# Layer 3 of a four-layer graph network: scaled rows and 512-column matmuls in place of scaled one-hots, radial weights per node tile

## The chip, the cores and the metric

The kernel runs on one core of a Trainium2 chip. The core has five engines with a queue of instructions each: TensorE (PE; its weight loads are shown apart as PEld), VectorE (DVE), ScalarE (ACT), GpSimd (POOL) and SyncE (SP), which here only issues DMAs. An engine executes its own queue in order and waits on semaphores for the others. Arrays live in the device's HBM; the engines work on SBUF (128 partitions) and PSUM (the matmuls' output). The metric is the time of one execution in microseconds (us), lower is better.

## The reference

A graph of 3125 nodes with 256 features and 50,000 edges, whose edges come sorted by target (`dst`), goes through four layers, each followed by a residual and a layer norm. Layers 0 (attention), 1 (attention over the graph, with a dense exponential) and 2 (two hypergraph convolutions) are not changed. Layer 3 is what the change rewrites:

```python
src = node_in[edge_src]
s0 = src[:, :MUL]                          # MUL = 64
s1 = src[:, MUL:].reshape(-1, MUL, 3)
a0 = edge_attr[:, 0:1]
a1 = edge_attr[:, 1:4]
out0 = alpha * (jnp.einsum('ei,io->eo', s0 * a0, w_00_0) + inv_sqrt3 * jnp.einsum('eim,em,io->eo', s1, a1, w_11_0))
out1 = alpha * (jnp.einsum('ei,io,em->eom', s0, w_01_1, a1) + jnp.einsum('eim,io->eom', s1 * a0[:, :, None], w_10_1))
msg_ang = jnp.concatenate([out0, out1.reshape(-1, 3 * MUL)], axis=1)
h = jax.nn.silu(edge_len_emb @ fc_w1 / np.float32(np.sqrt(10.0))) * np.float32(SILU_NORM)
msg_rad = h @ fc_w2 / np.float32(np.sqrt(64.0))
messages = msg_ang * msg_rad
agg = jax.ops.segment_sum(messages, edge_dst, num_segments=node_in.shape[0])
return agg / np.float32(np.sqrt(NUM_NEIGHBORS))
```

Each edge takes the row of its source node (one part of 64 features, three parts of 64), multiplies it with four numbers of the edge (`edge_attr`, 50,000 x 4) and with one number, the radial weight, that a small network makes of ten more (`edge_len_emb`, here `edge_attr_10`). Products of the row's parts with the four numbers go through 64 x 64 matrices and are added up over the edges of each target node. The matrices don't depend on the edge, so the sum can be taken first.

## The kernel before

**Node tiles and slots.** The 3125 nodes are 25 tiles of 128 (`NN = 25`). As edges are sorted by target, the edges of a node tile are a run that begins at a place read at run time (`self.at[t]`); the kernel takes `CAP = 2176` edges from there, as 128 partitions of `S = 17` slots. `one_hot` (L1002 to 1007) makes, for each slot, the 128 x 128 matrix that says which edge belongs to which node of the tile; a matmul with it as weights adds edges up over nodes.

**Gathers and fills.** `gather` (L86) is an indirect DMA that GpSimd issues: 128 rows of a table by an index per partition. A tile needs 17, in layer 0's attention (`kv`) as in layer 3 (`g`). `fill` (L1073) issues, also on GpSimd, scatters into `mat`, the matrix of edge counts of layers 1 and 2: 391 of them for the first of two matrices, eight per node tile inside the attention loop. They need only `put0` and `count`, which `counts` (L1010) makes, and the cleared matrix.

**What sets the order.** The code is one trace through Python; a planner then lays out each engine's queue. It estimates when an instruction's inputs and memory are ready and takes the earliest traced of those that are. So an instruction that is ready may go into the queue ahead of one that was traced before it. `attend` pins its gathers, the reads of `mine` and the first fill of each eight behind what was traced before them on GpSimd (`keep_in_program_order`, L1075 to 1082 and L1187 to 1194); the other seven fills of eight are not held by that, since two fills need no order between them. Memory is planned too: pools opened one after another share the same SBUF addresses, and a tile waits until those that lie on its place are done. `project_all`, `counts`, `edge_weights` and the attention of layer 0 are traced in this order (L1664 to 1667), and their pools share a region.

**Radial weights before.** `edge_weights` (L1558) calls `radial` (L119 to 143), which computes the radial weight of all 391 x 128 edges in one go, eight edge tiles at a time, and multiplies `edge_attr_4` with it:

```python
for i in range(n):
    nc.tensor.matmul(hp[:, i, :], emb[:, i * P:(i + 1) * P], w1, start=True, stop=True)
hs = sp.tile([P, B, F], F32, name="rad_h")
nc.scalar.activation(hs[:, :n], hp[:, :n], AF.Silu, scale=1.0 / math.sqrt(10.0))
nc.vector.tensor_mul(hs[:, :n], hs[:, :n], w2[:, None, :].to_broadcast([P, n, F]))
nc.vector.tensor_reduce(rad[:, j0:j0 + n], hs[:, :n], AX.X, ALU.add)
```

These are lines 136 to 141. The products are then turned by matmuls with the identity (L1570), copied (L1572) and stored as rows in HBM (`e_w4`, L1573), from where layer 3 loads 17 x 4 numbers per partition and tile (L1598).

**Layer 3 before.** Layer 2's last step writes each finished node tile into a table (`l3_tab`, by `l3_row`, L1579). Layer 3 gathers the 17 rows per partition of a tile (L1614 to 1616; three buffers `g3`), makes the one-hot (L1617, one buffer), and for each slot multiplies the one-hot on VectorE with each of the four weighted numbers (`ws`, L1622). Four matmuls per slot then use these as weights: one of 256 columns into `acc0` (L1624) and three of 128 columns into `acc1` (L1627), 640 columns in all. After 17 slots the sums are copied to SBUF (L1630, 1631), turned in five pieces (L1634), copied (L1636), multiplied with five blocks of the 64 x 64 matrices (`blk`, L1639), added to the residual (L1641, 1642), normed (`layernorm`, L1122) and stored (L1648).

**Attention in layer 0.** `attend` (L1173) gathers kv rows in halves of nine and eight slots (`fetch`, five buffers of 18.3 KB a partition), makes scores on PE and VectorE (L1222, 1224), reads back the scores of its nodes (`mine`, L1234), issues its fills, and after three tiles runs the feed-forward part (L1315).

Of the kernel before, what the change touches and what calls it, by code (L numbers as in the profile page):

```python
# [8 lines left out]
F32 = mybir.dt.float32  # L9
# [3 lines left out]
AF = mybir.ActivationFunctionType  # L13
# [5 lines left out]
P = 128  # L19
# [957 lines left out]
class Sorted(General):  # L977
# [580 lines left out]
    def edge_weights(self):  # L1558

        nc, tc = self.nc, self.tc  # L1560
        rows = self.dram.tile([EL, 4], F32, name="e_w4")
        with tc.tile_pool(name="ew", bufs=1) as cp, tc.tile_pool(name="ews", bufs=2) as sp, \
                tc.tile_pool(name="ewp", bufs=2, space=PSUM) as pp:
            w = cp.tile([P, NT, 4], F32, name="wts")
            self.radial(w)
            for c in range(LCH):
                n = min(P, NT - c * P)
                tp = pp.tile([P, 4, P], F32, name="w4_p")
                for i in range(4):
                    nc.tensor.transpose(tp[:n, i, :], w[:, c * P:c * P + n, i], self.ident)  # L1570
                o = sp.tile([P, P, 4], F32, name="w4")
                nc.scalar.copy(o[:n].rearrange("r p i -> r i p"), tp[:n])  # L1572
                nc.sync.dma_start(rows[c * P * P:(c * P + n) * P, :].rearrange("(r p) i -> r p i", p=P), o[:n])  # L1573
            z = cp.tile([ER - NT, P * 4], F32, name="zw")
            nc.vector.memset(z, 0.0)
            nc.sync.dma_start(rows[EP:, :].rearrange("(r p) i -> r (p i)", p=P), z)
        return rows
# [10 lines left out]
    def layer3(self, tab, rows, out):  # L1588
        nc, tc, a = self.nc, self.tc, self.a
        M = 64  # L1590
        alpha = 1.0 / math.sqrt(2.0 * M)
        with ExitStack() as at:
            pool = lambda n, b, **k: at.enter_context(tc.tile_pool(name=n, bufs=b, **k))
            cp, gp, sp, wp = pool("l3c", 1), pool("l3g", 3), pool("l3s", 2), pool("l3ws", 1)
            ap, pp = pool("l3a", 2, space=PSUM), pool("l3p", 1, space=PSUM)
            w4 = cp.tile([P, NN, S, 4], F32, name="w4_n")
            for t in range(NN):
                nc.sync.dma_start(w4[:, t], rows[bass.ds(self.at[t], CAP), :].rearrange("(p s) k -> p s k", s=S))  # L1598

            blk = cp.tile([P, 5, D], F32, name="blk")  # L1600
            nc.vector.memset(blk, 0.0)
            put = lambda i, half, col, n: nc.sync.dma_start(
                blk[half * M:(half + 1) * M, i, col * M:(col + 1) * M], a["L3_gnn_" + n])
            put(0, 0, 0, "w_00_0")
            put(0, 1, 1, "w_10_1")
            put(1, 0, 2, "w_10_1")
            put(1, 1, 3, "w_10_1")
            for m in range(3):
                put(2 + m, 0, 1 + m, "w_01_1")
                put(2 + m, 1, 0, "w_11_0")  # L1610
            nc.vector.tensor_scalar(blk, blk, alpha, None, op0=ALU.mult)
            nc.vector.tensor_scalar(blk[M:, 2:, :], blk[M:, 2:, :], 1.0 / math.sqrt(3.0), None, op0=ALU.mult)
            for t in range(NN):
# [3 lines left out]
                oh = self.one_hot(wp, t)  # L1617
                acc0 = ap.tile([P, D], F32, name="acc0")
                acc1 = ap.tile([P, 3, 2, M], F32, name="acc1")
                for s in range(S):  # L1620
                    ws = sp.tile([P, 4, P], F32, name="ws")
                    nc.vector.tensor_tensor(ws, oh[:, s, None, :].to_broadcast([P, 4, P]),  # L1622
                                            w4[:, t, s, :, None].to_broadcast([P, 4, P]), op=ALU.mult)
                    nc.tensor.matmul(acc0, ws[:, 0, :], g[:, s, :], start=(s == 0), stop=(s == S - 1))  # L1624
                    gb = g[:, s, :].rearrange("p (b c) -> p b c", c=M)
                    for m in range(3):
                        nc.tensor.matmul(acc1[:, m], ws[:, 1 + m, :], gb[:, 0:m + 2:m + 1, :],  # L1627
                                         start=(s == 0 and m == 0), stop=(s == S - 1 and m == 2))
                sums = sp.tile([P, 5, P], F32, name="sums3")
                nc.scalar.copy(sums[:, :2, :].rearrange("p a b -> p (a b)"), acc0)  # L1630
                nc.scalar.copy(sums[:, 2:, :], acc1.rearrange("p m b c -> p m (b c)"))
                tp = pp.tile([P, 5, P], F32, name="tp3")
                for i in range(5):
                    nc.tensor.transpose(tp[:, i, :], sums[:, i, :], self.ident)  # L1634
                st = sp.tile([P, 5, P], F32, name="st3")
                nc.scalar.copy(st, tp)  # L1636
                o = pp.tile([P, D], F32, name="o3")
                for i in range(5):
                    nc.tensor.matmul(o, st[:, i, :], blk[:, i, :], start=(i == 0), stop=(i == 4))  # L1639
# [5 lines left out]
                y = sp.tile([P, D], F32, name="y3")  # L1645
                self.layernorm(sp, y, x)
                n = min(P, N - t * P)
                nc.sync.dma_start(out[t * P:t * P + n, :], y[:n, :])  # L1648


    def run(self, out):
# [10 lines left out]
        with tc.tile_pool(name="w0", bufs=1) as self.wp:  # L1662
            qw = self.load_qkv(0)
            self.project_all(qw)  # L1664
            self.counts()
            rows = self.edge_weights()
            self.layer0(qw)
# [6 lines left out]
        with tc.tile_pool(name="xp", bufs=1) as xp:  # L1674
# [5 lines left out]
            self.layer3(tab, rows, out)  # L1680
# [159 lines left out]
```

## Time and profile before

| what | value |
|---|---|
| median of 3 runs | 5379.77 us (5369.6 to 5383.34) |
| the profiled execution | 5377.31 us, span of its profile 5375.0 us |
| granted PE clock, mean over the span | 0.843 |
| PE / DVE / ACT / POOL busy | 4066.3 / 2816.2 / 1385.3 / 2373.8 us |
| radial's matmuls (L137, 782) | 167.1 us, between 511 and 678 us |
| attention of layer 0, both passes | first kv gather at 765.7, last at 2928.5 us |
| layer 3 | first gather at 4761.0, last at 5357.8 us |
| DMA queue of GpSimd's indirect transfers | 115824 packets, 287.06 MB |

Busy time is the time in which an engine executes an instruction; waits, semaphores and the issuing of DMAs by SP and ACT are not counted. A row of a group of instructions reads: line, engine, operation, what it writes and reads, count, then busy time and mean length of one in ns, then the time that the engine stood idle just before them and what ended it. A row in order of time reads: start, length (us), engine, line, operation, tiles, count, and in brackets the idle time before. A row by stretches reads: the stretch, its length, busy time and count, granted clock, share of the DMA engines and GB/s. The chain of waits is followed back from the last instruction, at each step to what released it; "issue" is time in which the engine waited for nothing that the profile shows.

### The profile page before, as it was taken

To read this page: it belongs to the slowest core of one execution; us is meant where nothing else is said; L and a number is where in the kernel's file an instruction comes from. 1 tells how busy PE (TensorE), PEld (TensorE's weight loads), DVE (VectorE), ACT (ScalarE), POOL (GpSimd) and SP (SyncE) were. 2 spreads that over 40 slices of the span, in tenths; PEclk is the share of its full clock that TensorE was granted. 3 is DMA by queue.
4 is the path that set the end of the run, shared out by engine and by line. 5 is a ranking of instruction groups with operands and counts; after the bars stand their busy time and mean duration, and the time that the engine had idled before them with its cause. 6 is when DMAs were issued, how large, how long until landed. Compare 5 with 4: busy or idle time off the path is not lost. (4 is left out here: it accounts for less than half of the span.)

```text
span 5375.0 us, 59023 instructions
## 1 busy us (share of the span) xinstructions
PE 4066.3 (76%) x21215; PEld 2838.4 (53%) x21215; DVE 2816.2 (52%) x5251; ACT 1385.3 (26%) x2412; POOL 2373.8 (44%) x2116
## 2 busy tenths in 40 slices
PE   2631925557777776777777899897799999979998
PEld 1321914435555555556556643233466566568888
DVE  3424415436666656656667257988511211356665
ACT  1110101212222220222112257877652111100000
POOL 0001777764545517545554048787100000047776
PEclk9765556768888887788788679998999999989999
DMA  3244024234444426444554112221233333323333
GB/s 89 76 189 180 13 66 140 75 100 148 150 145 148 147 81 210 140 150 150 162 153 130 32 45 67 62 69 43 75 90 92 99 88 98 109 84 100 98 101 90
DMA packets 341121, 575.18 MB, mean 107 GB/s; under 512 B 101939, under 2 KB 238958, under 8 KB 340817
## 3 DMA queue, kind: packets, MB, share of 16 engines
q0 software_dynamic: 115824, 287.06, 18.5%
q1 hardware_dynamic: 219234, 243.28, 15.0%
q10 hardware_dynamic: 5760, 40.96, 1.9%
q8 instruction: 171, 2.80, 0.2%
q14 instruction: 132, 1.08, 0.1%
HBM read 485.82 MB, written 85.24 MB: 106 GB/s over the span
## 5 line engine op out<-in xcount | busy, mean ns | idle before, releaser
L87 POOL DMA_INDIRECT kv<-kv,src_i x850 | 933.7, 1098 | 695.8 <-issue 228.8
L1077 POOL DMA_INDIRECT mat<-count,put x782 | 907.9, 1161 | 509.7 <-DMA put<-put1d 231.6
L87 POOL DMA_INDIRECT g<-l_tab,src_i x425 | 469.0, 1103 | 1103.5 <-issue 1097.7
L1222 PE MATMUL qe<-q,oht 128*128 128x256 bf16 x2550 | 423.0, 316 | 431.1 <-DVE kv L1224 414.7
L1444 PE MATMUL acc<-e,xe 128*65 128x512 f32 (+2 forms) x1600 | 579.5, 516 | 80.9 <-DVE e L1441 80.6
L1222 PEld LDWEIGHTS <-oht 128*128 128x128 bf16 x2550 | 321.3, 147 | 590.9 <-issue 536.2
L1271 PE MATMUL acc<-kv,oh 128*128 128x264 f32 x1700 | 443.7, 424 | 65.3 <-DVE kv L1269 65.3
L1444 PEld LDWEIGHTS acc<-e,xe 128*65 128x65 f32 x1600 | 213.4, 141 | 436.8 <-issue 298.4
L1271 PEld LDWEIGHTS acc<-kv,oh 128*128 128x128 f32 x1700 | 354.9, 211 | 145.6 <-DVE kv L1269 76.5
L1495 PE MATMUL cv<-parts,m 128*128 128x512 bf16 x1250 | 411.4, 380 | 14.9 <-DMA m<-mat 14.7
L1495 PE MATMUL cv<-mids,m 128*128 128x512 bf16 x1250 | 408.4, 379 | 10.6 <-DVE y L1517 9.5
L1441 DVE TENSOR_TENSOR e<-e,m 128x1280 f32<-128x1280 f32 (+1 forms) x300 | 370.0, 1264 | 70.0 <-DMA m<-mat 54.6
L1495 PEld LDWEIGHTS <-m 128*128 128x128 bf16 x2500 | 244.7, 98 | 301.6 <-issue 16.1
L1622 DVE TENSOR_TENSOR ws<-oh,w_n 128x512 f32<-128x512 f32 x425 | 291.5, 691 | 159.7 <-PE acc L1627 153.6
L1224 DVE TENSOR_TENSOR kv<-kv,qe 128x512 f32<-128x512 f32 (+1 forms) x450 | 286.4, 648 | 168.6 <-DMA kv<-kv,src_i 140.5
L1627 PEld LDWEIGHTS acc<-g,ws 128*128 128x128 f32 x2550 | 352.7, 192 | 22.1
L1627 PE MATMUL acc<-g,ws 128*128 128x128 f32 x2550 | 354.1, 275 | 0.0
L1497 PE MATMUL cv<-mids,m 128*128 128x256 bf16 x1250 | 338.9, 273 | 0.0
L1497 PE MATMUL cv<-parts,m 128*128 128x256 bf16 x1250 | 338.6, 273 | 0.0
L1440 ACT ACTIVATE e<-e 128x1280 f32<-128x1280 f32 (+1 forms) x300 | 316.8, 1086 | 77.9 <-DVE e L1438 74.9
L1624 PE MATMUL acc<-g,ws 128*128 128x256 f32 x850 | 267.1, 396 | 47.2 <-DMA g<-l_tab,src_i 33.3
L137 PE MATMUL rad_p<-fc,emb 10*128 10x64 f32 x782 | 167.1, 416 | 163.3 <-DMA fc<-in_L_gnn_fc_w 163.3
(253 smaller groups left out, 5932.6 us busy)
## 6 DMA issues: line engine op xcount, KB each, us to landing
m<-mat SPq DMA_DIRECT2D x550, 160.0 KB
mat<-zmat ACTq DMA_DIRECT2D x40, 1000.0 KB
m<-mat SPq DMA_DIRECT2D x100, 320.0 KB
keys<-e_dst SPq DMA_DIRECT2D x50, 544.0 KB
q<-q SPq DMA_DIRECT2D x100, 192.0 KB
kv<-kv,src_i POOLq DMA_INDIRECT x850
kv<-qkv SPq DMA_DIRECT2D x50, 256.0 KB
mat<-count,put POOLq DMA_INDIRECT x782
```

What stands on the lines that cost most here:

```text
L87: return self.nc.gpsimd.indirect_dma_start(out=out, out_offset=None, in_=table, in_offset=bass.IndirectOffsetOnAxis(ap=idx, axis=0))
L1077: ins = nc.gpsimd.indirect_dma_start(out=self.mats[i], out_offset=bass.IndirectOffsetOnAxis(ap=put[:, j - j0:j - j0 + 1], axis=0), in_=sel ...
L1222: nc.tensor.matmul(qe[:, u, :], slots[:, h0 + s0 + u, :], q[:, k, :], start=(k == 0), stop=(k == 2))
L1224: nc.vector.tensor_mul(kv[:, s0:s0 + n, :D], kv[:, s0:s0 + n, :D], qe[:, :n, :])
L1271: nc.tensor.matmul(acc, oh[:, s, :], kv[:, s, D:], start=(h0 + s == 0), stop=(h0 + s == S - 1))
L1440: nc.scalar.activation(e[:, :R], e[:, :R], AF.Exp, scale=0.8)
L1441: nc.vector.tensor_mul(e[:, :R], e[:, :R], m[:, :R])
L1444: nc.tensor.matmul(accs[h, c][:, :n], xe[:, t, h, :], e[:, c:c + n], start=(t == 0), stop=(t == NN - 1))
L1495: nc.tensor.matmul(accs[i], block, parts[:, b, :2, :].rearrange("p a f -> p (a f)"), start=(b == 0), stop=False)
L1497: nc.tensor.matmul(accs[i][:, :D], block, parts[:, b, 2, :], start=False, stop=(b == NN - 1))
L1622: nc.vector.tensor_tensor(ws, oh[:, s, None, :].to_broadcast([P, 4, P]), w4[:, t, s, :, None].to_broadcast([P, 4, P]), op=ALU.mult)
L1627: nc.tensor.matmul(acc1[:, m], ws[:, 1 + m, :], gb[:, 0:m + 2:m + 1, :], start=(s == 0 and m == 0), stop=(s == S - 1 and m == 2))
```

## The change

- `edge_weights` becomes `edge_attributes`: radial is not called any more. `edge_attr_4` itself is turned and stored as rows (`e_attr`), and `edge_attr_10` is copied from HBM to a padded array in HBM (`e_emb`, ten rows).
- In layer 3 each node tile loads its own ten embedding rows, six times over with a shift of one edge, as 60 partitions of 2176 numbers, so that one matmul with a block-diagonal weight (`w1`, 60 x 6 x 64) gives the hidden layer of six slots; three such matmuls, three Silu, a product with `w2` and a reduction give the 17 radial weights per partition. They multiply the tile's `edge_attr` numbers.
- The gathered rows are scaled instead of the one-hots: ScalarE multiplies each slot's 256 features with the first number; VectorE forms the scalar part times the three others, and the three other parts times the three others, added up to one. The eight parts of 64 make a row of 512 columns (`y`), and one matmul per slot with the plain one-hot as weights adds it up.
- After the sum there are four pieces instead of five to be turned and multiplied.

```diff
-    def edge_weights(self):
-
-        nc, tc = self.nc, self.tc
-        rows = self.dram.tile([EL, 4], F32, name="e_w4")
+    def edge_attributes(self):
+
+        nc, tc, a = self.nc, self.tc, self.a
+        self.attr = self.dram.tile([EL, 4], F32, name="e_attr")
+        self.emb = self.dram.tile([10, EL], F32, name="e_emb")
+        run = EP // S
+        nc.sync.dma_start(self.emb[:, :EP].rearrange("r (s e) -> r s e", e=run),
+                          a["edge_attr_10"].rearrange("r (s e) -> r s e", e=run))
...
-            w = cp.tile([P, NT, 4], F32, name="wts")
-            self.radial(w)
+            w = cp.tile([P, NT, 4], F32, name="attr")
+            nc.sync.dma_start(w, a["edge_attr_4"])
...
-    def layer3(self, tab, rows, out):
+    def layer3(self, tab, out):
...
-            cp, gp, sp, wp = pool("l3c", 1), pool("l3g", 3), pool("l3s", 2), pool("l3ws", 1)
-            ap, pp = pool("l3a", 2, space=PSUM), pool("l3p", 1, space=PSUM)
-            w4 = cp.tile([P, NN, S, 4], F32, name="w4_n")
-            for t in range(NN):
-                nc.sync.dma_start(w4[:, t], rows[bass.ds(self.at[t], CAP), :].rearrange("(p s) k -> p s k", s=S))
+            cp, gp, yp, sp = pool("l3c", 1), pool("l3g", 3), pool("l3y", 2), pool("l3s", 2)
+            op = pool("l3o", 1)
+            ap, rp, pp = pool("l3a", 2, space=PSUM), pool("l3r", 2, space=PSUM), pool("l3p", 1, space=PSUM)
...
+            w1 = cp.tile([10 * U, U, F], F32, name="fc1")
+            nc.vector.memset(w1, 0.0)
+            for i in range(U):
+                nc.sync.dma_start(w1[10 * i:10 * (i + 1), i, :], a["L3_gnn_fc_w1"])
+            w2 = self.bcast(cp, a["L3_gnn_fc_w2"], F, "fc2")
...
-                oh = self.one_hot(wp, t)
-                acc0 = ap.tile([P, D], F32, name="acc0")
-                acc1 = ap.tile([P, 3, 2, M], F32, name="acc1")
+
+                emb = sp.tile([10 * U, CAP], F32, name="emb")
+                run = self.emb[:, bass.ds(self.at[t], CAP)]
+                nc.sync.dma_start(emb, bass.AP(tensor=run.tensor, offset=run.offset,
+                                               ap=[[1, U], [EL, 10], [1, CAP]]))
+                slots = emb.rearrange("k (p s) -> k s p", s=S)
+                hs = sp.tile([P, S, F], F32, name="rad_h")
+                for s0 in range(0, S, U):
+                    n = min(U, S - s0)
+                    hp = rp.tile([P, U, F], F32, name="rad_p")
+                    nc.tensor.matmul(hp[:, :n], slots[:10 * n, s0, :],
+                                     w1[:10 * n, :n, :].rearrange("k u f -> k (u f)"), start=True, stop=True)
+                    nc.scalar.activation(hs[:, s0:s0 + n], hp[:, :n], AF.Silu, scale=1.0 / math.sqrt(10.0))
+                nc.vector.tensor_mul(hs, hs, w2[:, None, :].to_broadcast([P, S, F]))
+                rad = sp.tile([P, S], F32, name="rad")
+                nc.vector.tensor_reduce(rad, hs, AX.X, ALU.add)
+                w4 = sp.tile([P, S, 4], F32, name="w4")
+                nc.sync.dma_start(w4, self.attr[bass.ds(self.at[t], CAP), :].rearrange("(p s) k -> p s k", s=S))
+                nc.vector.tensor_mul(w4, w4, rad[:, :, None].to_broadcast([P, S, 4]))
+
+                y = yp.tile([P, S, 8 * M], F32, name="y")
                 for s in range(S):
-                    ws = sp.tile([P, 4, P], F32, name="ws")
-                    nc.vector.tensor_tensor(ws, oh[:, s, None, :].to_broadcast([P, 4, P]),
-                                            w4[:, t, s, :, None].to_broadcast([P, 4, P]), op=ALU.mult)
-                    nc.tensor.matmul(acc0, ws[:, 0, :], g[:, s, :], start=(s == 0), stop=(s == S - 1))
-                    gb = g[:, s, :].rearrange("p (b c) -> p b c", c=M)
-                    for m in range(3):
-                        nc.tensor.matmul(acc1[:, m], ws[:, 1 + m, :], gb[:, 0:m + 2:m + 1, :],
-                                         start=(s == 0 and m == 0), stop=(s == S - 1 and m == 2))
+                    nc.scalar.activation(y[:, s, :D], g[:, s, :], AF.Copy, scale=w4[:, s, 0:1])
+                a1 = w4[:, :, 1:, None].to_broadcast([P, S, 3, M])
+                nc.vector.tensor_mul(y[:, :, 4 * M:7 * M].rearrange("p s (m c) -> p s m c", c=M),
+                                     g[:, :, None, :M].to_broadcast([P, S, 3, M]), a1)
+                s1 = g[:, :, M:].rearrange("p s (m c) -> p s m c", c=M)
+                nc.vector.tensor_mul(s1, s1, a1)
+                nc.vector.tensor_add(y[:, :, 7 * M:], s1[:, :, 0], s1[:, :, 1])
+                nc.vector.tensor_add(y[:, :, 7 * M:], y[:, :, 7 * M:], s1[:, :, 2])
+                oh = self.one_hot(op, t)
+                acc = ap.tile([P, 8 * M], F32, name="acc3")
+                for s in range(S):
+                    nc.tensor.matmul(acc, oh[:, s, :], y[:, s, :], start=(s == 0), stop=(s == S - 1))
```

`blk`, `sums`, `tp`, `st` and the output matmuls go from five pieces to four, and `run` calls `edge_attributes()` in place of `edge_weights()` and `layer3(tab, out)`.

## The prediction

> **What bounds the kernel now.** I read the page's groups by cost first, then the chain of waits over layer 3 (4755 to 5375 us), then the order of time at single instructions, and last the busy time by stretches, because the change takes work from one stage (507 to 690 us) and rebuilds another (4761 to 5375 us).
>
> In the groups, the gathers of layer 3 are the third largest group, and the scatters that fill `mat` the second; both are GpSimd (POOL) work. In layer 3's chain of waits GpSimd has nearly two thirds, and "issue", the 0.30 us between two of its instructions, most of the rest.
>
> ```profile
> L1077 POOL DMA_INDIRECT mat<-count,put x782 | 907.9, 1161 | 509.7 <-DMA put<-put1d 231.6
> L87 POOL DMA_INDIRECT g<-l_tab,src_i x425 | 469.0, 1103 | 1103.5 <-issue 1097.7
> ```
>
> ```profile
> by line: POOL g L87 64.6%; issue 20.0%; DMA g<-l_tab,src_i 7.7%; PE acc L1627 1.9%; PE acc L1624 1.7%; PE o L1639 0.8%; DVE ws L1622 0.5%; DVE oh L1005 0.4%; DMA l_tab<-y 0.3%; POOLq L1837 0.2%; DVE bn_st L104 0.1%; ACT st L1636 0.1%; ACT r
> ```
>
> So layer 3 is not a matmul stage, though PE is busy for 565 of its 593 us: PE follows the gathers. They start from 4760.99 to 5357.80, 424 steps of 1.407 us. An undisturbed one takes 0.95 us and 0.30 us of gap, 1.25 us; the rest, 597 - 530 = 67 us, is stalls. The order of time shows what a stall is:
>
> ```profile
> 4904.07 2.42 DVE L1005 TENSOR_TENSOR oh<-iota,key_n 128x2176 f32<-128x2176 f32 x1
> 4904.12 3.19 POOL L87 DMA_INDIRECT g<-l_tab,src_i  x1 [0.31 <-issue]
> ```
>
> ```profile
> 4893.04 0.69 DVE L1622 TENSOR_TENSOR ws<-oh,w_n 128x512 f32<-128x512 f32 x1 [0.41 <-PE acc L1627]
> 4893.15 1.40 POOL L87 DMA_INDIRECT g<-l_tab,src_i  x1 [0.30 <-issue]
> ```
>
> Both gathers end 0.82 us after the vector instruction in which they began. I take it as a rule that a gather beginning inside a VectorE instruction with two SBUF inputs waits for its end. Replayed over all 425 gathers with the recorded L1005 and L1622, it puts the last start at 5357.8, as recorded. The vector instruction itself isn't slowed (L1622 spans 672 to 747 ns).
>
> In front the bound is again GpSimd's queue:
>
> ```profile
> 764.42 0.96 POOL L1077 DMA_INDIRECT mat<-count,put  x1 [0.30 <-issue]
> 765.68 0.98 POOL L87 DMA_INDIRECT kv<-kv,src_i  x1 [0.30 <-issue]
> 770.99 0.69 DVE L1224 TENSOR_TENSOR kv<-kv,qe 128x512 f32<-128x512 f32 x1 [83.99 <-DMA kv<-kv,src_i]
> ```
>
> From 507 to 765 us GpSimd issues nothing but fills, and then the first kv gather of attention; VectorE has waited 84 us for it. Counting the fills (L1077) by stretches:
>
> ```profile
> 507.00:765.50 258.50, 199.39 (x194) 0.51 0.07 16
> 943.50:1158.00 214.50, 123.15 (x115) 0.68 0.26 77
> 1487.00:1878.00 391.00, 11.64 (x9) 0.84 0.47 145
> ```
>
> 194 fills lie ahead of attention. The second stretch holds three node tiles (three `mine` reads, L1234) and 115 fills, 71.5 us a tile; the third nine tiles and nine fills, 43.4 us a tile. In the second GpSimd has no gap, in the third it is idle about a third of the time. Why so many in front: the planner lets a fill go ahead of a gather that isn't ready. The kv buffers lie, in the program's memory plan, over the tiles of radial (the first over `wts`, `fc1`, `fc2` and `attr`), so they are free only when radial and its transposes end, near 690.
>
> **The change part by part.**
>
> *Front, removed.* radial's 782 matmuls (167.1 us), 49 Silu, 98 vector operations and 49 loads go. What stays of edge_weights (a load of 782 KB, 16 transposes, 4 copies, stores) took 7 us after `wts` was ready (682.5 to 689.3); the load ahead of it is bounded by 3 and 10 us. The kv buffers are then free near 507 + 17 = 524, with about 13 fills ahead of the first gather, which comes at 527 instead of 765.7: 239 us earlier. But the other 194 - 13 = 181 fills must still be issued. If the planner packs them as it did from 943 to 1158, 38 a tile, they lengthen 181/38 = 4.8 tiles by 71.5 - 43.4 = 28.1 us each, 134 us, which leaves 105; at 35 a tile (the stretch above held 41 kv gathers where three tiles need 51) 97. I take **-100 us**. Ends: 0 if fills are still put in front; -239 if all 181 (228 us at 1.26) fall into the time that GpSimd idles in the third stretch, 16 us a tile (391 less 192 of work and 171 gaps of 0.30, over nine). What hid the fills was radial; with that cover gone they cost gathers.
>
> *Front, added.* A copy of 2 MB from HBM to HBM, 11 to 26 us of transfer at the 76 to 189 GB/s seen before 507, queued on SP without inputs to wait for. Put early it hides behind the projections; with the eight small loads of layer 3's new constants and two early radial tiles on PE: **+3 us** (0 to 15).
>
> *Layer 3, matmuls.* A slot of 640 columns takes 1.10 us (4890.64 to 4891.74); 512 columns take 0.88 of it, 0.88 us, 15.0 us a tile for 18.7. Transposes and output matmuls fall from five to four (0.98 and 2.36 us a tile to 0.79 and 1.88); three radial matmuls of up to 384 columns add 2.0. PE: 19.7 us a tile instead of 22.0. Off the path, so worth nothing by itself.
>
> *Layer 3, VectorE.* From L1622 and L1005 (512 elements 0.691 us, 2176 elements 2.439) an element costs 1.05 ns and an instruction 0.15 us.
>
> ```profile
> L1622 DVE TENSOR_TENSOR ws<-oh,w_n 128x512 f32<-128x512 f32 x423 | 290.2, 691 | 159.7 <-PE acc L1627 153.6
> L1005 DVE TENSOR_TENSOR oh<-iota,key_n 128x2176 f32<-128x2176 f32 x24 | 58.5, 2439 | 0.8
> ```
>
> Gone are 17 `ws` (11.7 us). New are two products of 3264 elements (3.58 each), two additions of 1088 (1.30 each), the multiplication by `w2` (1.30), a reduction of 1088 (1.28, by the 685 ns of 512 in radial) and a product of 68 (0.22). With the one-hot (2.44) and 1.74 of norm and additions: 16.7 us a tile for 15.9. *ScalarE:* 17 scalings by 0.47 (a 256-wide scaling in layer 2), Silu 1.4, copies 1.2, square root 0.3, two table loads of 1.28 as Silu and square root alternate: 13.5 us. All three fit into a tile of 24 us or more.
>
> *Layer 3, gathers.* All that the 17 `ws` were in short pieces the two products and additions are in one block of 9.5 us, started when a tile's gathers land, while the next tile's are being issued. In it a gather passes only at an instruction's end: four in 9.5 us instead of one per 1.25, so 9.5 - 3.75 less up to 1.25 is lost, 4.5 to 5.8, say 4.8; times 24, 115 us. The one-hot costs 1.5 as now (36), the `w2` product about 0.3 (7). 158 less the 67 of now: **+91 us**, 27.8 us a tile. Replaying the rule with the new instructions and the one-hot in different places gives +51 to +122, and I keep these as ends.
>
> The Trainium skill, page "SBUF — State Buffer", section "Who interferes with whom", says that a vector instruction with two SBUF inputs contends with a GpSimd instruction that reads SBUF, but then that a probe saw `tensor_tensor` not stalling DMAs issued by GpSimd. By the second sentence layer 3 would run at 1.25 us a gather, 67 us faster than now; the rows above decide for the first.
>
> *Layer 3, end.* From the last gather's start to the span's end it is 17.2 us now, because PE has done 16 slots when the last lands. Then come 9.5 us of products and 15.0 us of matmuls in place of 1.5; one transpose, one output matmul and one copy less save 0.9; PE waking at a lower granted clock and an addition of the tile before in the queue cost some 3. **+25 us** (20 to 35).
>
> *New waits and who is behind them.* `oh` has one buffer and is now read by matmuls, so the next one-hot waits for a tile's last accumulation; behind it on VectorE wait the previous tile's norm and the next products. The 17 scalings wait for gathers on ScalarE, with `sums` and `st` behind. A gather needs its buffer back only three tiles later (80 us), so I cost these at nothing; if a buffer did come late, GpSimd would wait too. SP issues two loads a tile more, two tiles ahead.
>
> *Sum.* The profiled execution took 5377.3 (span 5375.0). 5377.3 - 100 + 3 + 91 + 25 = 5396; the median is 2.5 higher, so **5398 us**, +0.3%.
>
> **The rivals.**
> - *A, the front's gain is whole.* Fills fall into GpSimd's idle time: -239 instead of -100, 5259 us. For it: 1181 to 1878 has the room. Against: the planner packed 38 into a tile as soon as it could.
> - *B, the stalls don't grow.* Chunks of products are broken up by other waits, or fewer gathers fall into them: 0 instead of +91, 5307. Against: the replay's fit. A and B end on the other side; B decides if a tile stays at 23.9 us.
> - *C, the fills stay in front,* because something other than radial's memory holds the kv gathers: 0 instead of -100, 5498.
> - *D, a tile's chain takes the gathers' place.* PE's granted clock is 0.99 when it has no gaps, 0.84 to 0.87 from 1181 to 1878, where it is some 74% busy. At 0.65, as between 765 and 1158, 19.7 us become 30, 2.5 more than the gathers: +62 us, 5460. It decides from 27.8 us.
>
> **How the numbers follow.** Forecast 0.47, A 0.12, B 0.14, C 0.10, D 0.17. The forecast's own range is 5345 to 5450 (front 20, stalls 35 and end 8 either way, not all together). For 8 in 10 the range takes in B below and goes nearly to C above, leaving out A: 5290 to 5485. A measurement tells 0.3% (16 us) from no change. Faster (below 5364): A, B and 0.07 of the forecast, 0.33. Same: 0.19 of the forecast. Slower: the rest, 0.48.
>
> **What would show it.** Right: the first kv gather near 527, 30 to 40 fills a tile until about the eleventh tile, attention ending some 100 us earlier; in layer 3 a mean gather of about 1.3 us with maxima near 4.3, a tile every 27 to 29 us, GpSimd leading the chain; last gather to end about 42 us. Wrong: a first kv gather after 700 (C); fills under 20 a tile (A); gathers still 1.10 us in the mean (B); gathers that wait for `y` or `g`, with PE or VectorE leading layer 3's chain (D).

## The result and the profile after

The changed kernel takes 5436.73 us in the median of 4 runs (5421.72 to 5443.17), the kernel before 5378.49 beside it: ratio 1.0106, 95% interval 1.0082 to 1.0131. The change makes it 1.1% slower. Its profiled execution took 5436.5 us, with a span of 5434.7, 59.7 more than the span before.

Three moments of the trace split this difference (starts of instructions on GpSimd; "end" is the time from the start of the last gather of layer 3 to the end of the span; differences are taken before rounding):

| | before | after | difference |
|---|---|---|---|
| first kv gather of attention | 765.7 | 550.1 | -215.6 |
| last kv gather of attention | 2928.5 | 2856.9 | -71.6 |
| layer 3, first gather | 4761.0 | 4694.0 | -67.0 |
| layer 3, first to last gather | 596.8 | 696.3 | +99.5 |
| end | 17.2 | 44.3 | +27.2 |

The page's groups of the two big GpSimd instructions, for the kernel after:

```profile
L1077 POOL DMA_INDIRECT mat<-count,put x782 | 904.5, 1157 | 514.7 <-DMA put<-put1d 235.5
L87 POOL DMA_INDIRECT g<-l_tab,src_i x425 | 568.1, 1337 | 1106.4 <-DVE rad L1638 977.9
```

The fills cost what they did; a gather of layer 3 has gone from 1103 to 1337 ns in the mean. 425 x 0.234 = 99.5 us, the whole of layer 3's loss: the gathers didn't wait for anything, they became longer. The chain of waits over layer 3 (4694 to 5434 us) says the same, GpSimd still leads it:

```profile
by line: POOL g L87 52.3%; issue 15.2%; ACT y L1645 5.6%; DMA g<-l_tab,src_i 4.7%; DVE g L1650 3.3%; DVE y L1647 2.9%; DMA emb<-e_emb 2.3%; PE acc L1656 2.0%; PE o L1666 1.3%; DVE oh L1005 1.3%; ACT L1127 1.2%; PE rad_p L1633 1.2%; DVE rad_
```

VectorE's new work in layer 3, by groups of lines (line 1647 and 1650 are the two products, 1651 and 1652 the additions):

```profile
L1647 DVE TENSOR_TENSOR y<-g,w 128x3264 f32<-128x3264 f32 x25 | 89.0, 3558 | 296.6 <-DMA g<-l_tab,src_i 296.6
L1650 DVE TENSOR_TENSOR g<-g,w 128x3264 f32<-128x3264 f32 x25 | 88.7, 3550 | 13.1 <-ACT y L1645 13.1
L1005 DVE TENSOR_TENSOR oh<-iota,key_n 128x2176 f32<-128x2176 f32 x24 | 58.0, 2417 | 0.0
L1651 DVE TENSOR_TENSOR y<-g 128x1088 f32<-128x1088 f32 x25 | 32.2, 1289 | 0.6
L1652 DVE TENSOR_TENSOR y<-y,g 128x1088 f32<-128x1088 f32 x25 | 32.2, 1288 | 0.4
```

And one tile of it in order of time, VectorE and GpSimd:

```profile
5054.50 0.94 POOL L87 DMA_INDIRECT g<-l_tab,src_i  x1 [0.30 <-issue]
5055.00 3.56 DVE L1647 TENSOR_TENSOR y<-g,w 128x3264 f32<-128x3264 f32 x1 [14.12 <-DMA g<-l_tab,src_i]
5055.75 3.63 POOL L87 DMA_INDIRECT g<-l_tab,src_i  x1 [0.30 <-issue]
...
5060.66 3.54 DVE L1650 TENSOR_TENSOR g<-g,w 128x3264 f32<-128x3264 f32 x1
5060.93 4.09 POOL L87 DMA_INDIRECT g<-l_tab,src_i  x1 [0.30 <-issue]
```

The gather that begins at 5055.75 ends at 5059.38, 0.82 us after the product's end at 5058.56; the one at 5060.93 ends at 5065.02, again 0.82 us after its product. It is the stall of before, behind longer instructions. The gather at 5054.50, which began before the product, was on time.

The same trace has the counter-example. The reduction (L1638) has one input in SBUF and is as long as an addition; 23 gathers began inside it and none took more than 0.95 us. One of them:

```profile
5355.99 1.25 DVE L1638 TENSOR_REDUCE rad<-rad_h 128x17 f32<-128x1088 f32 x1
```

```profile
5356.35 0.95 POOL L87 DMA_INDIRECT g<-l_tab,src_i  x1 [0.30 <-issue]
```

Held until 0.82 us after the reduction, it would have taken 1.71. So a busy VectorE alone doesn't hold a gather.

In front, the first kv gather and VectorE's wait for it, and the busy time by stretches (up to the first kv gather; three tiles with many fills; a stretch with next to none):

```profile
548.88 0.96 POOL L1077 DMA_INDIRECT mat<-count,put  x1 [0.30 <-issue]
550.15 0.98 POOL L87 DMA_INDIRECT kv<-kv,src_i  x1 [0.30 <-issue]
...
555.47 0.69 DVE L1224 TENSOR_TENSOR kv<-kv,qe 128x512 f32<-128x512 f32 x1 [34.64 <-DMA kv<-kv,src_i]
```

```profile
507.00:549.90 42.90, 6.43 (x28) 4.78 (x29) 5.08 (x9) 4.09 (x4) 30.87 (x32) 0.54 0.16 46
784.00:944.00 160.00, 71.25 (x388) 55.87 (x389) 66.60 (x131) 19.21 (x37) 124.03 (x119) 0.67 0.31 91
1346.00:1800.00 454.00, 332.32 (x1890) 261.56 (x1890) 299.05 (x564) 109.95 (x203) 212.03 (x188) 0.84 0.46 141
```

32 fills lie ahead of attention instead of 194. The other 162 come back in its first eleven tiles: between the reads of `mine` the counts run 5, 13, 19, 38, 45, 32 as before, and then 67, 23, 20 and 58 where before had 3, 1, 1 and 1. Attention starts 216 us earlier and ends 72 us earlier.

### The profile page after: what moved, and what is told of

It is laid out like the page before. It is cut to its first block, busy times and chain, and to the rows that moved or that the text cites. A ratio compares the mean times of both kernels' runs of the same rounds, so it can differ in the third digit from the quotient of the medians.

```text
span 5434.7 us, 51896 instructions
## 1 busy us (share of the span) xinstructions
PE 3888.3 (72%) x17853; PEld 2432.8 (45%) x17958; DVE 2755.9 (51%) x4904; ACT 1616.0 (30%) x2879; POOL 2460.6 (45%) x2116
## 4 chain that ended last, share of the span: by engine, by line
PE 23%; POOL 11%; DVE 6%; issue 5%; DMA 3%; ACT 2%; SPq 0%; POOLq 0%; DVEq 0%; ACTq 0%
PE cv L1495 8%; POOL g L87 7%; PE cv L1497 5%; PE acc L1444 3%; POOL mat L1077 3%; DVE e L1441 1%; PE acc L1271 1%; PE w_p L1530 1%; PE el_p L1415 1%; DMA mat<-count,put 1%; ACT y L1645 1%; POOL kv L87 1%; PE mm L1335 1%; DMA g<-l_tab,src_i 1%; PE mm L1329 1%
## 5 line engine op out<-in xcount | busy, mean ns | idle before, releaser
L87 POOL DMA_INDIRECT g<-l_tab,src_i x425 | 568.1, 1337 | 1106.4 <-DVE rad L1638 977.9
L1656 PE MATMUL acc<-y,oh 128*128 128x512 f32 x850 | 393.9, 623 | 73.2 <-issue 30.7
L1495 PE MATMUL cv<-mids,m 128*128 128x512 bf16 x1199 | 394.5, 379 | 10.7 <-DVE y L1517 9.5
L1495 PE MATMUL cv<-parts,m 128*128 128x512 bf16 x1196 | 396.0, 380 | 0.3
L1495 PEld LDWEIGHTS <-m 128*128 128x128 bf16 x2500 | 244.8, 98 | 301.9 <-issue 16.2
L1247 DVE TENSOR_TENSOR mine<-mine,pen 128x320 f32<-128x320 f32 x50 | 24.6, 492 | 563.3 <-DMA mine<-scores,row 563.3
L1656 PEld LDWEIGHTS acc<-y,oh 128*128 128x128 f32 x850 | 169.6, 202 | 286.8 <-issue 234.3
L1256 PE MATMUL te<-top,oht 128*128 128x8 bf16 x2550 | 168.8, 201 | 172.6 <-ACT top L1360 162.8
L1497 PEld LDWEIGHTS <-m 128*128 128x128 bf16 x2500 | 244.7, 98 | 49.3 <-issue 14.5
```

What stands on the lines that cost most here:

```text
L87: return self.nc.gpsimd.indirect_dma_start(out=out, out_offset=None, in_=table, in_offset=bass.IndirectOffsetOnAxis(ap=idx, axis=0))
L1256: nc.tensor.matmul(te[:, s, :], slots[:, s, :], top3[:, k, :], start=(k == 0), stop=(k == 2))
L1495: nc.tensor.matmul(accs[i], block, parts[:, b, :2, :].rearrange("p a f -> p (a f)"), start=(b == 0), stop=False)
L1497: nc.tensor.matmul(accs[i][:, :D], block, parts[:, b, 2, :], start=False, stop=(b == NN - 1))
L1656: nc.tensor.matmul(acc, oh[:, s, :], y[:, s, :], start=(s == 0), stop=(s == S - 1))
```

## The experiments

The theory after the result (S and F): layer 3 lost its time to gathers that stand still while a VectorE instruction with two SBUF inputs runs, and the front gave back two thirds of its gain to fills that the planner puts ahead of gathers. The rivals: VectorE's load or a tile's chain sets layer 3's pace; radial per tile is what slows layer 3; the fills are harmless. "Total" is the median; ratios stand against the kernel before on the same chip.

| run | first kv | last kv | L3 first | L3 gathers | end | total | ratio (95%) |
|---|---|---|---|---|---|---|---|
| e1_psum | 551.7 | 2852.6 | 4690.8 | 580.7 | 42.8 | 5316.29 | 0.9882 (0.9862 to 0.9902) |
| e2_pin | 527.9 | 2754.2 | 4583.1 | 695.8 | 43.8 | 5332.06 | 0.9918 (0.9894 to 0.9942) |
| e3_front | 550.8 | 2846.8 | 4670.9 | 607.9 | 67.3 | 5362.85 | 0.9979 (0.9965 to 0.9992) |
| e4_oldfront | 766.3 | 2930.9 | 4768.3 | 696.2 | 45.4 | 5506.29 | 1.0233 (1.0213 to 1.0254) |
| b_pin | 690.5 | 2926.9 | 4758.9 | 598.5 | 17.2 | 5373.35 | 0.9962 (0.9948 to 0.9976) |
| e6_less | 552.8 | 2856.4 | 4696.1 | 616.7 | 29.0 | 5343.64 | one run |
| best1 | 528.8 | 2765.4 | 4597.4 | 576.3 | 42.5 | 5221.55 | 0.9682 (0.9666 to 0.9698) |
| best2 | 529.5 | 2683.8 | 4529.1 | 598.6 | 62.4 | 5178.78 | 0.9596 (0.9580 to 0.9612) |
| best4 | 527.7 | 2678.0 | 4516.7 | 551.9 | 39.1 | 5104.15 | 0.9489 (0.9469 to 0.9509) |

The kernel before took 5377.2 us beside the first four, 5395.5 beside the next four, 5378.4 beside the last.

**The two inputs (e1_psum).** The changed kernel, with the products' small operand in PSUM:

```diff
-                a1 = w4[:, :, 1:, None].to_broadcast([P, S, 3, M])
+                w4p = qp.tile([P, S, 3], F32, name="w4p")
+                nc.vector.tensor_copy(w4p, w4[:, :, 1:])
+                a1 = w4p[:, :, :, None].to_broadcast([P, S, 3, M])
```

> The changed kernel with one thing more: the three numbers of each edge are first copied into a PSUM tile (51 numbers a partition, two buffers), and the two products of 3264 elements read them from there, so that each has one input in SBUF instead of two. Order and length of VectorE's work stay (two products of about 3.56 us a tile, one copy of 0.2 us more). Theory S (a gather that begins inside a vector instruction with two SBUF inputs waits for its end): the two products stop no gather any more, only the one-hot, the two additions and the product with fc2 do. About 3.6 us a product less up to one gather's 1.25 us, so 2 to 4 us a tile and 24 tiles: layer 3's gathers take 48 to 96 us less (696 from first to last start becomes 600 to 648), the mean gather 1.15 to 1.25 us instead of 1.34, and the longest gather that begins in a product near 1 us instead of 4.1. Total 5340 to 5390 against 5437 of the changed kernel. Theory L (VectorE's load as such, or the chain of products, matmuls and output of a tile, sets the pace): nothing changes, 696 us and about 5437 stay, since VectorE has as much to do as before.

Measured: 5316.29 us, 580.7 us of gathers, both below the ranges that S gave. The order of time in that kernel:

```profile
4902.63 3.56 DVE L1650 TENSOR_TENSOR y<-g,w4p 128x3264 f32<-128x3264 f32 x1 [5.26 <-DMA g<-l_tab,src_i]
4903.41 0.95 POOL L87 DMA_INDIRECT g<-l_tab,src_i  x1 [0.30 <-issue]
4904.66 0.95 POOL L87 DMA_INDIRECT g<-l_tab,src_i  x1 [0.30 <-issue]
...
4906.62 3.55 DVE L1653 TENSOR_TENSOR g<-g,w4p 128x3264 f32<-128x3264 f32 x1
4907.16 0.94 POOL L87 DMA_INDIRECT g<-l_tab,src_i  x1 [0.30 <-issue]
...
4912.74 2.42 DVE L1005 TENSOR_TENSOR oh<-iota,key_n 128x2176 f32<-128x2176 f32 x1
4913.95 2.03 POOL L87 DMA_INDIRECT g<-l_tab,src_i  x1 [0.30 <-issue]
```

The products are as long as ever, 3.56 and 3.55 us, and gathers that begin inside them take 0.95 us. The one-hot, which still has two SBUF inputs, still holds its gather (ends 0.82 us after it). I added up, over the 425 gathers, what each took above 0.955 us, by the vector instruction that was running when it began: before 64 us (one-hot 35, `ws` 30), after 163 (products 132, one-hot 25, additions 7), here 47 (products 0, one-hot 32, additions 14, fc2 4; a gather just under 0.955 counts as negative in the totals, and small shares are left out). 163 - 64 = 99 us is the loss of layer 3. L falls: VectorE had as much to do. S stands, and my estimate of 2 to 4 us a tile was too low: 115.6/24 = 4.8 us came free.

**The fills (e2_pin, b_pin).** In e2_pin the changed kernel, in b_pin the kernel before, with the eight fills of a tile held:

```diff
-                    self.fill(0, self.put0[:, j:], j, j + FILL)
+                    with tc.issue_after(ins.ins):
+                        self.fill(0, self.put0[:, j:], j, j + FILL)
```

> The changed kernel, except that the eight fills of attention's tile that the program places behind the tile's read of its own rows are held there by an order, so that the planner can't bring them forward. Theory F (the front's gain is cut by fills that are put ahead of gathers: 32 ahead of the first kv gather, 60 and more in single tiles): the first kv gather comes at about 512 to 525 instead of 550, every tile of the first twelve takes 43 to 50 us, as the tiles with few fills do now, and the second tile pass begins 80 to 180 us earlier. Total 5260 to 5360. Rival H (fills in those tiles fill gaps of GpSimd that would be idle anyway, or the fills only move): attention ends within 20 us of where it ends now, total 5420 to 5450. If the planner makes GpSimd wait at the fills' places, it may be slower than 5437.

> The kernel before, with the eight fills of each attention tile held behind that tile's read of its own rows (the order that took the changed kernel from 5437 to 5332). Radial stays up front. Theory R (radial up front holds the kv gathers until its memory is free, near 690 us, and the 194 fills ahead of them only hid that): without fills ahead the first kv gather comes at 690 to 700 instead of 766, 163 to 172 us later than the 528 of the changed kernel with held fills, and this distance stays: layer 3's first gather at 4740 to 4760 against 4583 there, total 5350 to 5375, within 0.5% of the kernel before. Rival Q (the fills, not radial, held the kv gathers): first kv gather near 528, layer 3 from about 4590, total about 5205.

Measured: 5332.06 and 5373.35 us. GpSimd's first kv gather in e2_pin and in b_pin:

```profile
527.88 1.10 POOL L87 DMA_INDIRECT kv<-kv,src_i  x1 [66.11 <-issue]
```

```profile
690.45 1.10 POOL L87 DMA_INDIRECT kv<-kv,src_i  x1 [232.80 <-DMA e_w<-w]
```

With no fill ahead the changed kernel's first gather comes at 527.88. In b_pin it waits for radial's last store (`e_w4`, `e_w` in the row), until 690.45. So radial up front costs 162.6 us at the start, and 4758.9 - 4583.1 = 175.8 at layer 3, when no fills lie under it; and held fills alone give the kernel before next to nothing (-0.4%). Theory R holds, Q falls. In the changed kernel the fills' order is worth 4694.0 - 4583.1 = 110.9 us at layer 3, H falls; the total lies in F's range, the first gather 3 us behind it.

The price of a moved fill follows. After: 162 fills turn a lead of 215.6 us into 71.6, 144.0/162 = 0.89 us each. Held at eight a tile: 194 turn 237.8 (765.7 - 527.9) into 174.3 (2928.5 - 2754.2), 0.33 us each. In b_pin the same 194 turn 75.2 (765.7 - 690.5) into 1.6, 0.38 each. In a stretch with next to no fills GpSimd is busy 212 of 454 us; I read the two prices as fills that use this idle time when they are spread over the tiles, and don't fit in when they are bunched.

**The halves (e3_front, e4_oldfront).** e3_front has the new front and the radial weights per tile (with one PSUM buffer for `rad_p` instead of two), but the layer 3 of before; e4_oldfront has `radial` and `edge_weights` up front as before, and the changed layer 3 without its radial part:

```diff
-            rows = self.edge_weights()
+            self.edge_attributes()
...
+                nc.vector.tensor_mul(w4, w4, rad[:, :, None].to_broadcast([P, S, 4]))
                 oh = self.one_hot(wp, t)
```

```diff
-            nc.sync.dma_start(w, a["edge_attr_4"])
+            self.radial(w)
...
-                nc.vector.tensor_mul(w4, w4, rad[:, :, None].to_broadcast([P, S, 4]))
```

> Half of the change alone: radial up front is gone and radial weights are computed per node tile in layer 3, but layer 3 keeps its 17 weighted one-hots, its 640 columns and its five blocks. My account of the changed kernel (front -67 us at layer 3's start, gathers +100, tail +27) expects the first layer 3 gather 60 to 75 us earlier than in the kernel before, and about 5 to 15 us of new stalls from the product with fc2 and the reduction: total 5315 to 5335 against 5378 of the kernel before, ratio 0.988 to 0.992. Rival (the radial work per tile, with its loads, table changes and PE's three matmuls, is what slows layer 3): layer 3's gathers take 696 us here too, total about 5400 to 5410.

> The other half alone: layer 3 scales gathered rows and has one matmul of 512 columns per slot, but radial runs up front as in the kernel before, and the weights come ready from memory. My account: front 0, gathers +90 to +100 (the products' block without the product with fc2), tail +27: 5490 to 5505 against 5378 of the kernel before, ratio 1.021 to 1.024. Rival (radial per tile is what slows layer 3, or the two halves disturb each other): layer 3's gathers stay near 597 us, total 5380 to 5420.

e4_oldfront came at 5506.29, 1 us above the sum's range. Its 696.2 us of gathers are those of the changed kernel (696.3): radial per tile costs the gathers nothing there, and that rival falls. e3_front missed: 5362.85 instead of 5315 to 5335. (Its profile is the fastest of nine runs, 5347.86; they reach to 5378.41.) The front is there, with 90 us (4670.9) even more than the 60 to 75 expected, but the gathers lose 11 us and the end 50. The chain of waits over its layer 3, and the busy time of the stretch 4720 to 5280:

```profile
by line: PE acc L1655 42.1%; PE acc L1652 28.1%; PE o L1667 9.9%; PE rad_p L1635 8.1%; ACT L1637 3.6%; ACT rad_h L1637 1.9%; ACT sums L1659 1.6%; DMA emb<-e_emb 1.3%; issue 1.1%; DVE ws L1650 0.4%; DVE oh L1005 0.4%; ACT st L1664 0.2%; PE t
```

```profile
4720.00:5280.00 560.00, 544.13 (x3412) 477.90 (x3411) 389.21 (x584) 119.84 (x189) 429.49 (x391) 0.98 0.43 119
```

PE, busy 544 of 560 us at a granted clock of 0.98, leads: output matmuls of successive tiles begin 25.57 us apart (4953.29, 4978.86), the gathers come every 24.3 (607.9/25), and the difference piles up into the long end. The gathers' 11 us are gaps of 1.6 to 2.8 us before each of the last five tiles, where GpSimd waits for PE. So the shorter matmuls, which the prediction priced at nothing, make room on PE for radial's matmuls; the next run tests this.

**Relieving PE there (e6_less).** e3_front with the small matmuls of a slot cut to two, so that part of the sums is left out:

```diff
-                    for m in range(3):
+                    for m in range(2):
                         nc.tensor.matmul(acc1[:, m], ws[:, 1 + m, :], gb[:, 0:m + 2:m + 1, :],
```

> The half with the old layer 3 and the radial weights per tile (5346 us in its profiled execution, 608 us from first to last gather, 67 us from the last gather to the end), with the third of the three small matmuls of each slot left out: a part of the third direction's sums isn't computed and the fifth block is zero. Theory P (PE's matmuls, 25.6 us a tile there, have taken the gathers' place as the bound, so that PE is two tiles late at the end): PE has about 17 x 0.28 = 4.7 us a tile less, the gathers lead again at 595 to 602 us, and the end shrinks to 17 to 25 us: 5285 to 5305. Rival (the end is long because radial's chain of load, Silu, product, reduction and norm comes late in each tile): 67 us stay, about 5346.

Measured: the end falls from 67.3 to 29.0, not quite to P's 17 to 25, and the gaps before the last tiles are gone, so PE was what made the end long. But the gathers rise to 616.7 instead of falling: what they took above 0.955 us each adds up to 82 us instead of 63, and 136 gathers were held by over 0.1 us in a `ws` product instead of 56. Gathers and end together fall by 29.5 us, about half of the 48 to 63 that I expected. The total missed as well: 5343.64, the 5346 of the rival, because layer 3 also began 25 us later (4696.1 against 4670.9, in a single run on another chip). P is right about the end, and wrong that the gathers would be as quick as before. Why more of them meet a product I didn't follow up.

**Both repairs (best1).** The edits of e1_psum (with one buffer) and e2_pin together:

> The changed kernel with both repairs: fills held behind the tile's own read, and the three numbers of the products in one PSUM tile (one buffer). Layer 3 first gather at about 4583 as with held fills alone, gathers 581 us as with PSUM alone, end 43: 5205 to 5225, if the two stages are independent as my sum has it. Rival (the two gains share a cause, or a single PSUM buffer makes the products wait): above 5250.

Measured: 5221.55, ratio 0.9682, faster than both kernels. The single gains of 120.4 and 104.7 us add up to 225; together the repairs gave 215. Within these 10 us the two stages are independent.

**Further (best2, best3, best4).** best2 gives every long vector instruction but the additions one input in PSUM, issues the fills after the second half's gathers, moves the one-hot ahead of the products and cuts the last tile's products:

```diff
+            fixed = qp.tile([P, NN * S + F], F32, name="fixed")
+            keys = fixed[:, :NN * S].rearrange("p (t s) -> p t s", s=S)
+            w2p = fixed[:, NN * S:]
+            nc.vector.tensor_copy(keys, self.key)
...
+                oh = op.tile([P, S, P], F32, name="oh")
+                nc.vector.tensor_tensor(oh, self.iota[:, None, :].to_broadcast([P, S, P]),
+                                        keys[:, t, :, None].to_broadcast([P, S, P]), op=ALU.is_equal)
+                cuts = (0, S) if t < NN - 1 else (0, 6, 12, 15, S)
```

> The same, and further: the held fills are issued after the second half's gathers instead of before them; the one-hot's keys and fc2 are in PSUM too, so that of layer 3's long vector instructions only the two additions have two inputs in SBUF; and the last tile's products are cut into slots 0 to 5, 6 to 11, 12 to 14, 15 and 16, with its one-hot ahead of them. Theory S: the gathers lose the one-hot's 31 us and the fc2 product's 4 us: 540 to 552 us. End: only two slots' products and matmuls are left after the last landing, 20 to 28 us instead of 43. Front: 0 to 45 us earlier, as the second half's gathers no longer stand behind eight fills. Total 5110 to 5180. Rival (what I put down to the two inputs is the length of the instruction): the gathers stay at 575 to 585 us. Rival for the end (the chain of norm, transposes and output is what takes the time): 40 us stay.

Measured: 5178.78. The front gained 68 us over best1 at layer 3 (4597.4 to 4529.1), more than the 0 to 45 expected. The stalls fell to 15 us, as S has it, but the gathers as a whole took 598.6: GpSimd now stood still in eight gaps, each before a tile's first gather, 51 us in all, and the end grew to 62.4. Part of its chain of waits in order of time:

```profile
4808.41 6.79 ACT y L1651 x17
...
4815.21 0.34 SPq L1646
...
4815.79 9.26 DMA emb<-e_emb
...
4825.09 1.65 PE rad_p L1639 x2
```

After the 17 scalings a load of `w` (line 1646) goes, then behind it in SyncE's queue the load of radial's inputs, 9.26 us, and only then radial's matmuls. The chain of one tile has taken the gathers' place. best3 puts the one-hot back behind the products in all tiles but the last; best4 has four buffers for `w` as well:

```diff
+                if t < NN - 1:
+                    one_hot()
                 acc = ap.tile([P, 8 * M], F32, name="acc3")
...
-                w4 = sp.tile([P, S, 4], F32, name="w4")
+                w4 = sp.tile([P, S, 4], F32, name="w4", bufs=4)
```

> As the last kernel, but only the last tile has its one-hot ahead of the products; in the other 24 it stands behind them again, as in the changed kernel. There the gathers lost only 15 us to stalls but stood still for 51 us, and PE was three tiles late at the end (599 us of gathers, 62 us of end). Theory C (the early one-hot waits on VectorE for PE's last accumulation, and holds up the products and the radial weights queued behind it, so that a tile's chain took the gathers' place): with the old order the gathers take 540 to 555 us with no gap over 0.4 us, the end is 20 to 30 us, and the total is 0.948 to 0.952 of the kernel before. Rival G (at 22 us a tile PE or the loads of the radial inputs bind anyway): the gathers stay above 575 us and the total at 0.957 to 0.962.

> The same kernel as best3, again: there the kernel before took 6308 us on that chip instead of 5377 to 5396, with every DMA-fed stage longer, so that run tells neither theory from the other. Theory C: gathers 540 to 555 us with no gap over 0.4 us, end 20 to 30 us, total 0.948 to 0.952 of the kernel before. Rival G: gathers above 575 us, total 0.957 to 0.962.

> The kernel of best2 beside it on the same chip, so that the place of the one-hot is the only difference. As before: gathers near 599 us with gaps of about 51 us in all, end near 62 us, total 0.958 to 0.961 of the kernel before; theory C has it 45 to 75 us slower than best3b, rival G within 10 us of it.

> best3 with four buffers instead of two for the small tile w of numbers per edge. In best2 and best3 the chain of layer 3 ran through SyncE's queue: the load of the next w waits for a buffer that is free only after all 17 scalings of a tile, and the load of radial's inputs (9 us) stands behind it; so radial's weights come late in each tile. Theory Q (this queue is what took the gathers' place): gathers 540 to 560 us with no gap over 0.4 us, end 20 to 30 us, 0.945 to 0.953 of the kernel before on an undisturbed chip. Rival G (PE or the single one-hot buffer binds at 24 us a tile): gathers above 575 us, end above 45 us, ratio 0.957 to 0.962. If the kernel before takes about 6300 us on the chip again, the run decides neither.

best3, best3b and best2b decide nothing: the chips that they ran on gave 6308, 6303 and 6303 us to the kernel before, and ratios of 0.9772 (0.9742 to 0.9802), 0.9757 (0.9717 to 0.9797) and 0.9798 (0.9754 to 0.9842). best2b came 22.5 us behind best3b beside it, between the 45 to 75 of theory C and the 10 of rival G. best4 came on a chip like the first ones: 5104.15 us, ratio 0.9489, gathers 551.9 with no gap above 0.4 us. SyncE's waits for the load of `w`, first best2, then best4 (line waiting, what it waited for: us in total, times, longest):

```profile
SPq L1646 <- ACT y L1651: 94.2, 22, 22.8
```

```profile
SPq L1646 <- ACT y L1651: 13.0, 1, 13.0
```

The wait is nearly gone and the gathers lead again, as Q forecast; G falls. But two edits lie between best2 and best4, the place of the one-hot (C) and the buffers of `w` (Q), and which of them gave how much stays open. The end missed, 39.1 instead of 20 to 30: PE is still at the previous tile's matmuls until about 5077.5, the last tile's one-hot begins at 5077.59, and PE's last 34 matmul instructions start at 5081.50, with the products all but done before the one-hot. The one-hot's single buffer would explain its late start, but VectorE had no idle time before it, so that isn't shown.

## Why the prediction came out as it did

It said 5398 us, +0.3%; it is 5436.7, +1.1%. The sign and the range were right, and the mechanisms were those of the forecast; the sum was some 40 us low, 30 of them in one term. The sign was in part luck: the forecast stood 18 us above the kernel before, hardly more than the 16 us that it took for no change, and its two large terms, -97 and +91, were both off towards slower.

- *Front, -97 with the added copy: measured -67.0 at layer 3.* This is the mis-sized term. The step "the kv buffers are then free near 524, the first gather at 527" is right: with held fills it is 527.88. "About 13 fills ahead" was wrong, 32 were issued first, and that alone is 22 us at the start. The 162 that remained cost 0.89 us each; the prediction's 139 us for 181 come to 0.77. Another 4.6 us go between the end of attention and layer 3. The cause was named ("What hid the fills was radial; with that cover gone they cost gathers") and two runs show it: holding the fills back gains 105 us without radial in front (e2_pin) and 22 us with it (b_pin, beside its own 5395.5).
- *Layer 3's gathers, +91: measured +99.5.* Right in mechanism and nearly in size. The block of products and additions cost 139 us of stalls, 5.8 a tile, the prediction's upper end, where 4.8 was taken; the one-hot cost 25 instead of 36 and the product with fc2 1 instead of 7. The longest gather took 4.17 us (4.3 was forecast). The block was set too short: by the prediction's own lengths two products and two additions are 9.76 us, not 9.5 (9.69 measured), which makes 4.8 to 6.0 us a tile by its formula.
- *End, +25: measured +27.2.* The products began at 5393.82 and the 17 matmul pairs ran from 5407.54 for 15.10 us. Between them lay the last tile's one-hot, 2.42 us behind the additions in VectorE's queue, which the prediction hadn't counted.
- *The rule behind +91* was argued from two rows and a replay; e1_psum shows it by taking one input out of SBUF, with a copy of 0.2 us a tile as the only other change. It needs one more condition, the start. Of the gathers of both kernels that began inside an instruction with two SBUF inputs and more than 0.14 us before its end, all 237 that began 0.046 us or more after its start were held, and all 15 that began in its first 0.03 us took 0.94 to 0.95. That is why the product with fc2 cost 1 us: of 31 gathers at it, 8 began with it and 18 in its last 0.1 us. The Trainium skill, page "SBUF — State Buffer", section "Who interferes with whom", says that a vector instruction with at most one SBUF input doesn't contend with GpSimd (outside some modes), and that one with two contends with GpSimd's reads. The runs agree on both, 0.95 us against 4.09. For the indirect DMAs of this kernel they don't bear out the same section's remark that `tensor_tensor` was seen not to stall DMAs.
- *The rivals.* A (fills fall into idle time) was nearest to what e2_pin makes of the kernel, with 174 us of lead left at attention's end instead of 239; the kernel as written doesn't do it. B would have needed 0 instead of +99.5. C falls with the first gather at 550. D didn't occur in the changed kernel, where no gather waited for a buffer and the granted clock was 0.83 over layer 3's gathers, but a tile's chain did take the gathers' place in two of its relatives, through PE in e3_front (at a clock of 0.98, so not for D's reason) and, as its chain of waits reads, through SyncE's queue in best2.
- *Slips in the working.* 512 columns are 0.8 of 640, not 0.88; the 0.88 us a slot behind it is right (15.10 us measured for the last tile's 17). The row by stretches gives 0.67 for the clock between 765 and 1158, not 0.65, by which D would have cost about 40 us instead of 62.

## What to carry to other kernels

Where GpSimd's gathers set the pace, look at VectorE's long instructions with two SBUF inputs before counting engine time: joining 17 short ones into two long ones and two additions cost 99 us here, and a small operand put into PSUM made the two long ones harmless. Before a stage is taken from in front of a queue, count what fills that queue meanwhile, since it has to go somewhere; spread it by an explicit order rather than leave it to the planner. When one bound is lifted, check the next two, PE's busy time per tile and the order of loads in a shared queue, for they were within 1 to 2 us a tile of the gathers here.

## What the hardware showed that I had not expected

With one input in PSUM the stall doesn't shrink, it vanishes: 0 of the 132 us are left, and the product takes 3554 ns instead of 3558. The kernel before took 6303 to 6308 us on two chips, 17% more than on the others; in best3's trace there a gather of layer 3 is as quick as ever (973 ns), but GpSimd stands still for 221 us in 14 gaps, each before a tile's first gather. In the longest, 36.2 us up to 5484.97, ScalarE and VectorE begin nothing before 5458.19 either, after 70.0 and 61.6 us without work, so the hold-up isn't GpSimd's own; what they waited for the trace doesn't name.
